# A two-layer graph network on one core: when x is loaded, and in how many transfers x, z and the output move

## The chip, the cores and the metric

The kernel runs on one core of one Trainium2 chip. The metric is the device time of one execution in microseconds. The time of a kernel is the median of several runs. Profiles come from one further execution that the hardware profiler records, and that execution can be longer than the timed ones.

## The reference, cut to what matters

There are 32 batches of x, each of 512 nodes by 512 features in float32, and one adjacency matrix `adj` of 512 x 512 for all of them.

```python
h = relu(layernorm(x))
x = x + einsum('nm,bmd->bnd', adj, h) @ W0 + b0          # layer 0
h = relu(layernorm(x))
q, k, v = h @ Wq + bq, h @ Wk + bk, h @ Wv + bv            # 8 heads of 64
scores = q @ k.T / 8 + (1 - adj) * -1e9                    # layer 1
x = x + (softmax(scores) @ v) @ Wo + bo
```

The mask of layer 1 uses weighted edges: an entry of `adj` that is not exactly 1 costs up to 1e9. So each row's softmax is, in float32, a choice of the one node with the largest entry, unless two entries are nearly equal. The kernel tests this at the start on the chip and takes `single_path` when it holds, `general_path` otherwise. The profile shows `single_path`.

## The kernel before, in words

In `single_path` layer 1 becomes: for each node take the row of h of the node that its mask selects, and multiply it by the folded weight Wv Wo (`wvo`). Many nodes select the same one, so only the distinct selected rows are computed, at most 352 (`32 * S`, S = 11).

Each 512 x 512 product is done by `product`, a Strassen-Winograd scheme of seven block products. Their pieces are named p1, p5, u2, c11, c22, c12, c21, in that order. A piece is four matmuls into a PSUM bank (line 287), and after each piece a `take` function moves the bank on: `take_onto` adds it to x on VectorE (line 344), `take_new` copies it on ScalarE (line 326) or adds it on VectorE (line 324), and `take_z` uses ScalarE (line 337) and VectorE (line 334). Pieces p1, u2, c22 and c21 share one bank, so c22 can't begin before u2 has been taken.

The order is written out by hand. For each b of the loop there are 21 steps, one for each piece of three products: steps 0 to 6 are layer 0 of batch b, steps 7 to 13 the aggregation with `adj` of batch b+1, and steps 14 to 20 layer 1 of batch b-1. `put(batch, step, f)` hangs a small piece of work on a step. All engines run in the order in which this loop emits their instructions, and an engine's queue stands still while its head waits.

Work around the change, for a batch n:

- `load_x` reads x of batch n into one of five buffers of x (`xs[n % 5]`), so batch n+5 needs the buffer of n after n was stored. It is issued by SyncE.
- `ln0` normalizes x for layer 0 (`stats` is line 194, `power` line 201 on GpSimd, `offset` line 204, `relu` line 212).
- After layer 0, the halves of x are normalized for layer 1 (steps 6 to 10), and `put_h` writes h to DRAM (`hs`, line 488, SyncE).
- `get_h` (line 494, GpSimd) gathers the listed rows of `hs` into `hc`, eleven indirect transfers: three at step 12 and eight at step 15, of which most run in the next pass of the loop.
- `transpose_h` (line 529) and `layer1` produce `zs`, the layer's output by columns.
- `put_z` transposes `zs` into `zr` on VectorE (line 545), in two parts, and SyncE writes each part to DRAM (`z`) in four transfers, one for each quarter of the partitions (line 549). Part (6, S) is put at step 20, part (0, 6) at step 0 of the next pass.
- `finish` (line 553, GpSimd) gathers for each node its row of `z` and adds it to x in the transfer itself, four indirect transfers at step 1.
- `store` (line 559) writes x to the output at step 12, in four transfers.

A tile framework adds the semaphores. The transfers of SyncE use eight semaphores in turn, and each transfer waits until the one eight places before it, which had the same semaphore, has landed. A reader of a tile waits for all the transfers that wrote it.

At the end, batch 31's layer 1 is done for all its rows by `layer1_rows` (lines 507 to 523). The last `finish` and the store of batch 30, issued by ScalarE, close the program.

Of the kernel before, what the change touches and what calls it, by code (L numbers as in the profile page):

```python
# [17 lines left out]
P = 128  # L18
# [8 lines left out]
def gnn_two_layers(ctx: ExitStack, tc: tile.TileContext, x, adj, w0, b0, wq, bq, wk, bk, wv, bv, wo, bo, out):  # L27
# [149 lines left out]
    with tc.If(single > P - 1) as cmp:  # L177
        single_path(tc, x, wv, bv, wo, bo, out, kept)
# [38 lines left out]
def single_path(ctx: ExitStack, tc: tile.TileContext, x, wv, bv, wo, bo, out, kept):  # L217
# [14 lines left out]
    nc = tc.nc  # L232
    B, N, D = x.shape
    C, DC = N // P, D // P
# [12 lines left out]
    X, H0 = {0: xs[0], 1: xs[1]}, {0: hs[0], 1: hs[1]}  # L247
    H0S, H1, HS, HC, HT, HTS, Z, ZT, ZR = {}, {}, {}, {}, {}, {}, {}, {}, {}

    def load_x(b):  # L250
        X[b] = xs[b % 5]
        for c in range(C):
            nc.sync.dma_start(X[b][:, c, :], x[b, c * P:(c + 1) * P, :])


    def blk(t, chunks, cols, half=HALF):
# [284 lines left out]
    def put_z(b, s0, s1):  # L541
        if b not in Z:
            Z[b] = dram.tile([32 * S, D], F32, name="z")
            ZR[b] = work.tile([P, S, P], F32, name="zr")
        nc.vector.transpose(ZR[b][:, s0:s1, :].rearrange("p s (c e) -> p s c e", c=4),
                            ZT[b][:, :, 32 * s0:32 * s1].rearrange("p c (s j) -> p s c j", j=32))
        rows = Z[b].rearrange("(s j) (q f) -> q j s f", j=32, q=4)
        for q in range(4):
            nc.sync.dma_start(rows[q][:, s0:s1, :], ZR[b][32 * q:32 * q + 32, s0:s1, :])

    def finish(b):
        for c in range(C):
# [1 line left out]
                out=X[b][:, c, :], out_offset=None, in_=Z[b],  # L554
                in_offset=bass.IndirectOffsetOnAxis(ap=place[:, c:c + 1], axis=0), compute_op=ALU.add)

    def store(b, eng=nc.sync):
        for c in range(C):
            eng.dma_start(out[b, c * P:(c + 1) * P, :], X[b][:, c, :])

    def run(steps, work_by_step):
        if steps is None:
# [16 lines left out]
    with tc.manual_schedule():  # L579
# [6 lines left out]
        for b in range(B + 1):  # L586
            todo = [[] for _ in range(21)]

            def put(batch, step, f, *args):
                if 0 <= batch < B:  # L590
                    todo[step].append(lambda: f(batch, *args))

            put(b - 2, 15 if b == B - 1 else 1, finish)
            put(b + 2, 2, load_x)
            for step, i in ((0, 0), (1, 1), (2, 2), (3, 3)) if b > 0 else ((1, 0), (2, 1), (2, 2), (3, 3)):
                put(b + 1, step, h0_sum, i)
            put(b - 2, 14 if b == B - 1 else 0, put_z, 0, 6)
            if b == B - 1:
                put(b - 2, 13, put_z, 6, S)
# [22 lines left out]
            if b < B - 1:  # L622
                put(b - 2, 12, store)
            elif b == B:
                put(b - 3, 1, store)
# [13 lines left out]
            if b < B and b != B - 2:  # L639
                put(b - 1, 20, put_z, 6, S)  # L640
# [36 lines left out]
                run(layer1(b - 1) if b < B and b != B - 2 else None, todo[14:21])  # L677
        layer1_rows(B - 1)
        if B > 1:
            store(B - 2, nc.scalar)  # L680


@with_exitstack
# [261 lines left out]
```

## Time and profile before

| what | value |
|---|---|
| time, median of 3 runs | 1118.38 us (1115.33 to 1119.31) |
| span of the profiled execution | 1168.3 us (its time: 1170.05 us) |
| TensorE matmul / VectorE / ScalarE / GpSimd busy | 94% / 78% / 31% / 56% |
| mean granted TensorE clock | 0.984 |
| HBM read / written | 96.28 MB / 89.46 MB |
| DMA queue of SyncE | 102320 packets, 123.05 MB, 31.0% of the 16 engines' span |
| DMA queue of GpSimd | 29472 packets, 56.47 MB, 27.4% |

A busy share is averaged over the whole span. The profile's chain follows back, from the last instruction, what each one waited for. In a timeline each row is a run of equal instructions: start, length, engine, line, operation, what it writes and reads, and in brackets how long the engine was idle before it and what ended that. TensorE's ends are modelled. In a windows answer each row is one stretch, with the busy time of each engine, then the granted clock, the mean busy share of the 16 DMA engines, and GB/s.

For one batch in the middle (it begins at 564.5 us of the span), SyncE's timeline is: eight transfers of z from 565.11, four of x from 568.95, two of hs from 582.78, four of the output from 585.31.

### The profile page before, as it was taken

How to read it: one execution, taken by the hardware profiler on the slowest of the kernel's cores; microseconds unless marked ns; L12 is line 12 of the kernel's file. 1: busy time of each engine (PE TensorE's matmuls, PEld its weight loads, DVE VectorE, ACT ScalarE, POOL GpSimd, SP SyncE). 2: the span in 40 equal slices, each digit the busy share in tenths (PEclk: the TensorE clock that was granted, in tenths of full speed). 3: DMA queues.
4: the chain of work that ended last, by engine and by line, in shares of the span. 5: the costliest groups of instructions: out<-in, count | busy, mean ns of one | idle time of the engine just before them, and what ended most of it. 6: DMA issues, size and time to landing. Idle time of an engine off the chain costs nothing.

```text
span 1168.3 us, 15855 instructions
## 1 busy us (share of the span) xinstructions
PE 1100.6 (94%) x5408; PEld 957.8 (82%) x5408; DVE 905.7 (78%) x1859; ACT 359.4 (31%) x655; POOL 653.9 (56%) x584
## 2 busy tenths in 40 slices
PE   7999989999989999999999999899999999999885
PEld 3658878989978989888989888798998889998782
DVE  6879868878867878787888888687887878887760
ACT  4223313233313233323323332223333232233120
POOL 2146536655646765565765555566565656666443
PEclk9999989999989999999999999999999999999998
DMA  6414665655666665576665657566566756666438
GB/s 225 153 19 129 165 173 140 171 170 149 168 173 139 165 180 147 153 191 167 150 177 171 159 155 187 133 170 178 155 165 172 190 140 167 180 176 156 120 118 203
DMA packets 135146, 186.90 MB, mean 160 GB/s; under 512 B 17472, under 2 KB 61120, under 8 KB 135056
## 3 DMA queue, kind: packets, MB, share of 16 engines
q1 hardware_dynamic: 102320, 123.05, 31.0%
q0 software_dynamic: 29472, 56.47, 27.4%
q10 hardware_dynamic: 3264, 6.29, 1.5%
q8 instruction: 44, 0.72, 0.2%
q14 instruction: 46, 0.38, 0.1%
HBM read 96.28 MB, written 89.46 MB: 159 GB/s over the span
## 4 chain that ended last, share of the span: by engine, by line
PE 83%; DVE 6%; issue 3%; POOL 3%; ACT 1%; DMA 1%; another core or an unknown queue 1%; SPq 0%; POOLq 0%; ACTq 0%; DVEq 0%
PE mm L287 78%; DVE x L344 2%; POOL x L553 1%; PE mm L139 1%; PE mm L480 1%; PE mm L371 1%; DVE st L194 1%; DMA x<-in_x_dram 1%; PE mm L520 1%; ACT h L212 1%; POOL rstd L201 1%; POOL hc L494 1%; DVE h0s L266 1%; DVE yT L324 0%
## 5 line engine op out<-in xcount | busy, mean ns | idle before, releaser
L494 POOL DMA_INDIRECT hc<-hs,listed x341 | 356.2, 1045 | 261.9 <-DMA hs<-h 157.2
L344 DVE TENSOR_TENSOR x<-mm,x 128x512 f32<-128x512 f32 x217 | 149.6, 690 | 146.6 <-PE mm L287 107.7
L326 ACT COPY yT<-mm 128x512 f32<-128x512 f32 x124 | 71.8, 579 | 614.3 <-PE mm L287 478.3
L553 POOL DMA_INDIRECT x<-z,place x124 | 196.0, 1581 | 70.2 <-issue 47.9
L287 PE MATMUL mm<-w_t,sel 128*128 128x256 f32 x744 | 182.2, 396 | 37.9 <-DVE x L344 31.6
L212 ACT ACTIVATE h<-x,off,rstd 128x512 f32<-128x512 f32 x256 | 194.7, 807 | 48.2 <-DVE off L204 46.3
L287 PEld LDWEIGHTS mm<-w_t,sel 128*128 128x128 f32 x744 | 143.9, 196 | 67.5 <-DVE x L344 39.4
L201 POOL TENSOR_TENSOR rstd<-ve,mhalf 128x2 f32<-128x2 f32 (+1 forms) x97 | 97.2, 1002 | 156.9 <-DVE ve L200 151.8
L194 DVE BATCH_NORM_STATS2 st<-x 128x6 f32<-128x512 f32 x256 | 171.6, 670 | 8.4 <-DMA x<-in_x_dram 7.3
L287 PE MATMUL mm<-adjT_s,h0s 128*128 128x256 f32 x744 | 170.9, 379 | 0.4 <-ACT yT L326 0.2
L287 PEld LDWEIGHTS mm<-adjT_s,h0s 128*128 128x128 f32 x744 | 141.2, 190 | 20.3 <-ACT yT L326 1.2
L287 PE MATMUL mm<-hTs,wvo_t 128*128 128x176 f32 x720 | 117.8, 313 | 1.7 <-ACT zs L337 1.7
L287 PE MATMUL mm<-w_s,yT 128*128 128x256 f32 x496 | 117.2, 379 | 0.0
L287 PE MATMUL mm<-adjT,h 128*128 128x256 f32 x496 | 117.2, 379 | 0.0
L337 ACT ACTIVATE zs<-mm,cvo_c 128x176 f32<-128x176 f32 x248 | 87.4, 404 | 94.7 <-PE mm L287 60.4
L287 PEld LDWEIGHTS mm<-hTs,wvo_t 128*128 128x128 f32 x720 | 109.7, 190 | 2.8 <-ACT zs L337 2.8
L287 PEld LDWEIGHTS mm<-adjT,h 128*128 128x128 f32 x496 | 94.2, 190 | 13.2 <-issue 0.5
L287 PEld LDWEIGHTS mm<-w_s,yT 128*128 128x128 f32 x496 | 93.1, 190 | 11.7 <-issue 0.5
L458 DVE TENSOR_TENSOR x<-x,b_r 128x512 f32<-128x512 f32 x128 | 86.5, 677 | 0.0
L287 PE MATMUL mm<-hT,wvo 128*128 128x176 f32 x480 | 81.4, 313 | 0.0
L287 PEld LDWEIGHTS mm<-hT,wvo 128*128 128x128 f32 x480 | 75.3, 190 | 1.5
L324 DVE TENSOR_TENSOR yT<-mm,yT 128x512 f32<-128x512 f32 x93 | 63.5, 682 | 4.1 <-PE mm L287 2.7
(152 smaller groups left out, 1262.9 us busy)
## 6 DMA issues: line engine op xcount, KB each, us to landing
hs<-h SPq DMA_DIRECT2D x64, 512.0 KB
out_dram<-x SPq DMA_DIRECT2D x124, 256.0 KB
x<-in_x_dram SPq DMA_DIRECT2D x120, 256.0 KB
z<-zr SPq DMA_DIRECT2D x124, 96.0 KB
z<-zr SPq DMA_DIRECT2D x124, 80.0 KB
hc<-hs,listed POOLq DMA_INDIRECT x341
x<-z,place POOLq DMA_INDIRECT x124
x<-in_x_dram ACTq DMA_DIRECT2D x4, 256.0 KB
```

The lines of the kernel that those rows point to most:

```text
L139: nc.tensor.matmul(ps, hs[0][:, m, d * P:(d + 1) * P], adjT[:, m, :], start=(m == 0), stop=(m == C - 1))
L194: self.nc.vector.bn_stats(st, self.src[:, self.chunks[i], :])
L201: self.nc.gpsimd.tensor_tensor(self.rstd, ve, self.mhalf[:, 0:n], ALU.pow)
L212: self.nc.scalar.activation(dst, src, AF.Relu, bias=self.off[:, i:i + 1], scale=self.rstd[:, i:i + 1])
L287: nc.tensor.matmul(bank[:, m, 0:half], lhs[:, k, m * P:(m + 1) * P], rhs[:, k, :], start=(first and m == 0 and k == 0), stop=(k == 1), ski ...
L324: nc.vector.tensor_add(dst, bank, dst)
L326: nc.scalar.copy(dst, bank)
L337: nc.scalar.activation(dst[:, m, :], bank[:, m, :], AF.Identity, bias=cvo_c[:, 2 * i + m:2 * i + m + 1])
L344: nc.vector.tensor_add(dst, bank, dst)
L458: nc.vector.tensor_add(X[b][:, c, :], X[b][:, c, :], b0_r)
L494: nc.gpsimd.indirect_dma_start(out=HC[b][:, s, :], out_offset=None, in_=HS[b].rearrange("n (q d) -> (n q) d", q=4), in_offset=bass.Indirec ...
L553: nc.gpsimd.indirect_dma_start(out=X[b][:, c, :], out_offset=None, in_=Z[b], in_offset=bass.IndirectOffsetOnAxis(ap=place[:, c:c + 1], axi ...
```

## The change

Three things change, all in transfers that SyncE issues. No arithmetic changes.

- x of a batch is loaded at step 15 of pass b for batch b+3, behind the store of batch b-2, whose buffer it takes. Before, it was loaded at step 2 of pass b for batch b+2. Batches 2 and 3 are still loaded at step 2 of passes 0 and 1.
- A load of x, and a store of the output, is one transfer of 1 MB instead of four of 256 KB. The last store, by ScalarE, keeps four (`store_rows`).
- z is written in four transfers of 176 KB, after the second transpose, instead of four of 80 KB after the first and four of 96 KB after the second.

It is meant to read x at a time when the transfers are few, to have it long before it is needed, and to have fewer transfers and fewer semaphores to wait for.

```diff
     def load_x(b):
         X[b] = xs[b % 5]
-        for c in range(C):
-            nc.sync.dma_start(X[b][:, c, :], x[b, c * P:(c + 1) * P, :])
+        nc.sync.dma_start(X[b], x[b].rearrange("(c p) d -> p c d", p=P))
...
-        rows = Z[b].rearrange("(s j) (q f) -> q j s f", j=32, q=4)
-        for q in range(4):
-            nc.sync.dma_start(rows[q][:, s0:s1, :], ZR[b][32 * q:32 * q + 32, s0:s1, :])
+        if s0 == 0:
+            for q in range(4):
+                nc.sync.dma_start(Z[b].rearrange("(s j) (q f) -> q j s f", j=32, q=4)[q], ZR[b][32 * q:32 * q + 32])
...
-    def store(b, eng=nc.sync):
-        for c in range(C):
-            eng.dma_start(out[b, c * P:(c + 1) * P, :], X[b][:, c, :])
+    def store(b):
+        nc.sync.dma_start(out[b].rearrange("(c p) d -> p c d", p=P), X[b])
+
+    def store_rows(b):
+        for c in range(C):
+            nc.scalar.dma_start(out[b, c * P:(c + 1) * P, :], X[b][:, c, :])
...
-            put(b + 2, 2, load_x)
+            if b < 2:
+                put(b + 2, 2, load_x)
+            if b > 0:
+                put(b + 3, 15, load_x)
...
-            store(B - 2, nc.scalar)
+            store_rows(B - 2)
```

## The prediction

> **What bounds the kernel now.** I read the page's busy shares first, then the chain of waits, then the timelines of PE, POOL and SP over single batches, last the windows of one batch for the DMA share.
>
> ```profile
> PE 1100.6 (94%) x5408; PEld 957.8 (82%) x5408; DVE 905.7 (78%) x1859; ACT 359.4 (31%) x655; POOL 653.9 (56%) x584
> ...
> PE 83%; DVE 6%; issue 3%; POOL 3%; ACT 1%; DMA 1%; another core or an unknown queue 1%; SPq 0%; POOLq 0%; ACTq 0%; DVEq 0%
> ```
>
> TensorE is the bound: 94% busy and 83% of the chain. DMA is 1% of the chain, so no transfer sets the end directly. A change of transfers can only win what TensorE loses in waits. How much is that? One batch of the steady state is layer 0 of b, aggregation of b+1 and layer 1 of b-1. In the PE timeline a batch begins where w_s,yT follows layer 1:
>
> ```profile
> 216.60 1.89 PE L287 MATMUL mm<-w_s,yT 128*128 128x256 f32 x8
> ...
> 249.14 1.89 PE L287 MATMUL mm<-w_s,yT 128*128 128x256 f32 x8
> ...
> 258.58 3.00 PE L287 MATMUL mm<-w_t,sel 128*128 128x256 f32 x8 [2.37 <-DVE x L344]
> ...
> 285.99 1.89 PE L287 MATMUL mm<-w_s,yT 128*128 128x256 f32 x8
> ```
>
> Batch 5 takes 249.14 - 216.60 = 32.54 us and has no PE gap: that is the floor. Batch 6 takes 36.85 us, with a gap of 2.37 us at c22, which waits until DVE has taken u2 (L344). Batch 1 starts at 74.66 and batch 31 at about 1103.8. The 29 whole batches between would need 29 x 32.54 = 943.7, and batch 30, which has no layer 1, about 24.2: 967.9 in all, against 1029.1 in the trace. So 61 us of the profiled run are waits. But that run took 1170.05 us where the timed ones took 1118.4. Taking out the waits gives 1170.05 - 61.2 = 1108.9, so the timed runs can hold only some 9.5 us of such waits, 0.3 us a batch, if start and end are the same. Most of the L344 waits seem to belong to the profiled execution. This 9.5 us is the most that the loop can give.
>
> The waits that may be left are found in the loop through GpSimd. It is nearly as long as the batch:
>
> ```profile
> 570.19 0.95 POOL L494 DMA_INDIRECT hc<-hs,listed  x1 [0.31 <-issue]
> 572.60 1.58 POOL L553 DMA_INDIRECT x<-z,place  x1 [1.46 <-DMA x<-in_x_dram]
> 574.49 1.55 POOL L553 DMA_INDIRECT x<-z,place  x1 [0.30 <-issue]
> 576.34 1.54 POOL L553 DMA_INDIRECT x<-z,place  x1 [0.30 <-issue]
> 578.19 1.53 POOL L553 DMA_INDIRECT x<-z,place  x1 [0.30 <-DVE ve L200]
> 579.18 1.29 POOL L201 TENSOR_TENSOR rstd<-ve,mhalf 128x2 f32<-128x2 f32 x1
> ...
> 588.43 1.05 POOL L494 DMA_INDIRECT hc<-hs,listed  x1 [5.37 <-DMA hs<-h]
> ```
>
> In batch 15 (from 564.6) the eleven gathers of hc end at 571.14, the four of finish follow, and behind them in POOL's order stands rstd (L201), whose input ve was ready at 577.98. From rstd the path goes to off, relu, hs, its landing, the gathers at 588.43 and so back to finish. ACT shows how tight it is:
>
> ```profile
> 580.76 0.81 ACT L212 ACTIVATE h<-x,off,rstd 128x512 f32<-128x512 f32 x1 [1.38 <-DVE off L204]
> 581.48 0.57 ACT L326 COPY yT<-mm 128x512 f32<-128x512 f32 x1
> 581.95 0.81 ACT L212 ACTIVATE h<-x,off,rstd 128x512 f32<-128x512 f32 x1
> 582.66 0.57 ACT L326 COPY yT<-mm 128x512 f32<-128x512 f32 x1
> ```
>
> The take of u2 (582.66 to 583.23) stands behind the relu that waited for rstd, and c22 of the aggregation begins at 583.77: 0.5 us of slack. The reader is to see that 0.5 us more at finish reaches TensorE, and that finish waits 1.46 us (0.3 would be its plain spacing) for z.
>
> **Where the DMA engines are full.** Windows of the same batch (DMA share and GB/s are the last two columns):
>
> ```profile
> 564.45:567.45 3.00, 3.00 (x17) 2.66 (x16) 3.00 (x5) 0.71 (x2) 2.08 (x4) 1.00 0.42 110
> 567.45:570.45 3.00, 3.00 (x16) 2.64 (x15) 1.66 (x3) 0.00 (x0) 2.39 (x3) 1.00 0.86 222
> 570.45:573.45 3.00, 3.00 (x15) 2.40 (x14) 1.98 (x3) 0.00 (x0) 1.54 (x2) 1.00 1.02 316
> ...
> 590.00:597.16 7.16, 7.16 (x51) 7.16 (x50) 6.87 (x15) 5.05 (x10) 6.03 (x6) 1.00 0.18 47
> ```
>
> z is written and x read at 0.86 to 1.02 of the engines, just when finish waits, while during layer 1 they stand at 0.18. The change carries 1 MB from the full stretch to the empty one.
>
> **What the Trainium skill says.** "DMA: Bandwidth & Descriptors", Anatomy of one DMA: about 2 us of each transfer are fixed, most of it the receipt of the write, HBM being slowest. The trace agrees roughly: the last z issue begins at 568.47, and finish was held until after 571.14. "Perfetto Trace Analysis", Tensor Engine Instruction: the end of a matmul in a profile is an estimate from its size. That fits: PE stands back to back while DVE waits for its result for 2 us and more. "TensorE: Matmul & The Clock Gate", HAM oscillation: an idle stretch can halve the clock for a window. The mean granted clock of 0.984 shows a little of it, so a wait of TensorE removed may save somewhat more than itself.
>
> **The change part by part.**
>
> Load of x. Of b+2 at step 2 before; of b+3 at step 15 after, so some 20 us earlier for each batch. DVE's waits for x are 7.3 us in 5 places, all before 22 us, where this load plays no part. The earlier arrival is worth 0 by itself. The load now stands behind the store whose buffer it takes (b+3 and b-2 share one of five), so SyncE waits there for the store to land. Behind it in SyncE's order is only z of the next batch, due 13 us after the store is issued (585.3 to about 599). A store of 1 MB behind hs took until about 590, and 1 MB of x at the 320 GB/s of the third window takes another 3.3 us: done near 594. Cost 0. It crosses the hc gathers of layer 1, paced by GpSimd at 1.25 us each, with 8 us until their transpose needs them: 0.
>
> One transfer for x and one for output. Six issues of 0.45 us fewer on SyncE, whose time is free: 0. The four stats wait for all of x instead of a quarter: 0 with 20 us in hand. The store waits for all four finish gathers; the last is issued at 578.19 and has landed well before the store at 585.3: 0.
>
> Four for z. Before, issues run from 565.11 (after the first transpose of zr) to 568.91. After, the first can go only when the second transpose ends, 566.55, and the fourth at about 566.6 + 3 x 0.45 = 568.0, done at 568.4: 0.5 us sooner than the eighth. The data, 704 KB, are 1408 packets of 512 B; the packet records have a median of 27 ns for these (84 for 2 KB), so 88 x 27 ns = 2.4 us on 16 engines alone and about 3.0 beside the hc gathers. From a first packet near 567.5 this ends at 570.5, and lands near 571; before, it was paced by the issues. So z is ready between 0.5 us earlier and, if the burst runs at the pace of before (704 KB at about 160 KB/us, 4.4 us), 1.0 us later. I take 0.3 us earlier. GpSimd then also waits for four z semaphores instead of eight, two waiting instructions of 0.09 us fewer. With x no longer filling the engines, the gathers of finish and their receipts are quicker. Together finish starts about 0.5 us sooner, which is as much as the 0.3 us a batch that the loop can give. I take 0.25 us x 29 = 7 us.
>
> The end. z of batch 30 is the last long link: eight issues from 1137.51 to 1142.3, held up by lanes and by finish of batch 29, then 4.99 us of idle on POOL before finish at 1149.29, and the stores follow. With four issues from 1138.92 to about 1140.7 the last is 1.6 us sooner; the engines are full there, so I take 1.3. Sum: 1118.4 - 7 - 1.3 = 1110.
>
> **The rivals.**
>
> Hidden anyway. x was never late and finish is not what TensorE waits for in timed runs; only the end gains, 1118.4 - 1.3 = 1117. For it: DMA is 1% of the chain, and the lost time of the trace stands at L344, which names PE and DVE, no transfer. Batch 30 loads no x and still has a c22 gap (3.45 us at 1084.74), so x is not its cause. Against it: the tight loop above.
>
> Slower: the burst of z. z starts 1.5 us later and lands 1.0 us later; finish, rstd, relu and the takes all move, and beyond 0.5 us of slack TensorE waits: 0.4 us x 29 = 12 us less the 1.3 of the end, 1129. A milder form, 0.2 us a batch, gives 1123. For it: z is the first link of that path and the first half loses its head start. Against it: the issues, not the engines, paced z before (0.42 and 0.86 of the engines).
>
> Much faster: the L344 waits of the profile are in timed runs too and come from full DMA engines. 61 us would be at stake, but 1118.4 leaves room for 9.5; the lowest time I believe is 1108.9 - 1.3 - some start effects, about 1102 to 1107.
>
> **How the numbers follow.** Forecast 0.45 and much faster 0.05, both faster; hidden 0.27; burst 0.23, most of it over 0.5% slower. Faster by over 0.5% is under 1112.8, slower is over 1124.0. Hence 0.5, 0.27, 0.23. The range is 1102 to 1127: below, all waits gone; above, half the weight of the burst is still inside.
>
> **What would show it.** In the profile after: the idle before the first finish gather falls from about 1.3 to under 1 us and DMA share in layer 1 rises from 0.18 to about 0.6; stats still wait for no x; POOL's idle at the end falls from 4.99 to about 3.5. L344 waits may stay, since they are the profiled run's. I am wrong if finish starts later than 8 us after the batch's begin, if rows of adjT_s,h0s wait for ACT yT, or if the L344 waits vanish and the timed run falls under 1102.

## The result, and the profile after

The kernel after takes 1123.81 us (median of 4 runs, 1122.38 to 1124.36), the kernel before 1118.65 us beside it. The ratio is 1.005, with an interval of 1.0028 to 1.0073: slower by half a per cent. A second measurement (f1 below) gave 1.0055 (1.0042 to 1.0068). The ratios and intervals in this document leave out executions that took over 1.5% more than the fastest of their kernel, which concerns the runs named e and one execution of h3, while each time is the median of all.

The profile before can't be laid beside the profile after as it stands. It is of an execution of 1170 us, when the timed ones took 1118; the profile after (span 1122.6 us) agrees with its timed runs. A further profile of the kernel before, called g1 (1114.3 us, span 1112.6), has the level of the timed runs, so the comparison is made with g1. It is a single execution at the quick end of them. The kernel after is one line shorter above `product`, so its L286, L325, L343 and L552 are L287, L326, L344 and L553 of the kernel before.

The page of after, its busy shares and its chain by engine, and the chain of g1:

```profile
PE 1089.8 (97%) x5408; PEld 950.7 (85%) x5408; DVE 904.9 (81%) x1859; ACT 359.0 (32%) x655; POOL 662.2 (59%) x584
...
PE 73%; DVE 13%; POOL 6%; DMA 3%; issue 3%; ACT 1%; SPq 0%; POOLq 0%; ACTq 0%; DVEq 0%
```

```profile
PE 82%; DVE 8%; POOL 4%; issue 2%; DMA 1%; ACT 1%; SPq 1%; ACTq 0%; POOLq 0%; DVEq 0%
```

TensorE is still the bound, 97% busy. But the chain passes through it less (73% against 82% in g1), and more through DVE, POOL and DMA: other engines set more often when TensorE goes on. One batch from TensorE's timeline, batch 15 again:

```profile
540.71 1.89 PE L286 MATMUL mm<-w_s,yT 128*128 128x256 f32 x8
...
573.73 1.89 PE L286 MATMUL mm<-w_s,yT 128*128 128x256 f32 x8
```

It takes 33.02 us, 0.48 more than the floor of 32.54. The median of the 29 batches is 33.01 (32.69 in g1). So most batches are a little late; the latest takes 34.17 us. What starts it, as the runs below show, is z. SyncE's timeline of this batch:

```profile
542.68 2.45 SPq L548 DMA_DIRECT2D z<-zr  x4
```

The first z issue is 1.97 us after the batch's begin, where before it was 0.51 us after it. The windows of the batch show what the DMA engines do then (DMA share and GB/s last), in after and then in g1:

```profile
540.70:543.70 3.00, 3.00 (x16) 2.67 (x15) 3.00 (x5) 0.70 (x2) 2.16 (x3) 1.00 0.18 53
543.70:546.70 3.00, 3.00 (x15) 2.64 (x15) 2.12 (x4) 0.00 (x0) 2.47 (x2) 1.00 0.93 230
546.70:549.70 3.00, 3.00 (x16) 2.65 (x15) 1.53 (x4) 0.00 (x0) 2.08 (x2) 1.00 0.34 88
566.10:573.26 7.16, 7.16 (x50) 7.16 (x49) 6.88 (x15) 5.08 (x11) 5.88 (x6) 1.00 0.68 204
```

```profile
536.40:539.40 3.00, 3.00 (x16) 2.64 (x15) 3.00 (x5) 0.70 (x2) 2.19 (x3) 1.00 0.47 124
539.40:542.40 3.00, 3.00 (x15) 2.66 (x14) 2.12 (x5) 0.00 (x0) 2.43 (x2) 1.00 0.90 216
542.40:545.40 3.00, 3.00 (x15) 2.64 (x14) 1.53 (x4) 0.00 (x0) 2.66 (x2) 1.00 0.96 297
561.90:569.06 7.16, 7.16 (x50) 7.16 (x49) 6.83 (x14) 5.05 (x10) 5.76 (x6) 1.00 0.13 41
```

x has gone to layer 1, as meant: 0.68 of the engines there, where it was 0.13. The third stretch of the batch has fallen from 0.96 to 0.34. But the first has fallen too, from 0.47 to 0.18, and z now fills the second at 0.93: the engines stand nearly empty while z is held back for the second transpose, and then all of z has to pass at once. By the semaphore records of this batch z's four transfers land 4.37, 5.54, 6.22 and 7.52 us after its begin; in g1 the last of eight lands at 6.43. Over all batches the medians of the last landing are 7.19 and 6.88 us. GpSimd's timeline shows the consequence:

```profile
546.78 1.42 POOL L493 DMA_INDIRECT hc<-hs,listed  x1 [0.30 <-issue]
549.04 1.58 POOL L552 DMA_INDIRECT x<-z,place  x1 [0.84 <-issue]
550.93 1.55 POOL L552 DMA_INDIRECT x<-z,place  x1 [0.30 <-issue]
552.78 1.54 POOL L552 DMA_INDIRECT x<-z,place  x1 [0.30 <-issue]
554.63 1.53 POOL L552 DMA_INDIRECT x<-z,place  x1 [0.30 <-DVE x L343]
555.62 1.29 POOL L201 TENSOR_TENSOR rstd<-ve,mhalf 128x2 f32<-128x2 f32 x1
```

The gathers of `hc` are over at 548.20. `finish` could follow at the plain spacing of 0.30 us, and starts 0.54 us later than that. The bracket says "issue", but z is what it is held for: its last transfer has landed 0.81 us earlier. The same stretch of the kernel before, in g1 (batch from 536.38):

```profile
542.44 1.43 POOL L494 DMA_INDIRECT hc<-hs,listed  x1 [0.30 <-issue]
544.17 1.58 POOL L553 DMA_INDIRECT x<-z,place  x1 [0.31 <-DMA x<-in_x_dram]
...
549.76 1.53 POOL L553 DMA_INDIRECT x<-z,place  x1 [0.30 <-DVE ve L200]
550.74 1.31 POOL L201 TENSOR_TENSOR rstd<-ve,mhalf 128x2 f32<-128x2 f32 x1
```

In this batch of g1 there is no wait for z at all. In the next one there is:

```profile
577.49 1.59 POOL L553 DMA_INDIRECT x<-z,place  x1 [1.10 <-DMA x<-in_x_dram]
```

(The bracket names x, whose transfers use the same semaphores; z's last transfer has landed 0.85 us earlier.) Of the 28 batches with a `finish`, 13 in g1 wait for z beyond the plain spacing, 7.0 us in all; in after all 28 do, 13.3 us in all. The wait of 1.46 us in the profile before came of an execution in which the gathers of `hc` ended earlier in the batch (6.5 us after its begin, not 7.5). Behind the four gathers stands rstd (L201). DVE had written its input ve at 553.91 in the batch of after, and it begins at 555.62 (its record overlaps that of the last gather; spans of GpSimd are rough). The Trainium skill says why ("PSUM — Partial Sum Buffer", Engine vs sequencer instructions): GpSimd's queue is a strict FIFO. The trace agrees; these 1.7 us are the gathers ahead of it (1.2 in the batch of g1). ScalarE's timeline carries the delay on:

```profile
557.20 0.81 ACT L212 ACTIVATE h<-x,off,rstd 128x512 f32<-128x512 f32 x1 [1.89 <-DVE off L204]
557.91 0.56 ACT L325 COPY yT<-mm 128x512 f32<-128x512 f32 x1
558.38 0.81 ACT L212 ACTIVATE h<-x,off,rstd 128x512 f32<-128x512 f32 x1
559.10 0.57 ACT L325 COPY yT<-mm 128x512 f32<-128x512 f32 x1
```

and so do the weight loads of TensorE (PEld):

```profile
559.72 1.59 PEld L286 LDWEIGHTS mm<-adjT_s,h0s 128*128 128x128 f32 x8 [0.25 <-ACT yT L325]
561.33 1.70 PEld L286 LDWEIGHTS mm<-adjT,h0s 128*128 128x128 f32 x8
563.54 1.59 PEld L286 LDWEIGHTS mm<-adjT_s,h 128*128 128x128 f32 x8 [0.51 <-DVE yT L323]
```

The take of u2, at 559.10, stands behind the relu that waited 1.89 us (1.35 in the batch of g1), and piece c22 waits for it. How closely TensorE follows can be read from after alone: batches in which `finish` begins at 7.90, 8.41 and 9.44 us take 32.58, 33.11 and 34.17 us. Over its 28 batches each microsecond by which `finish` begins later goes with 0.92 us more of batch. The waits of the whole run, total us, times, longest, in after:

```profile
ACT h L212 <- DVE off L204: 78.5, 64, 3.0
DVE off L204 <- POOL rstd L201: 61.2, 66, 2.2
...
PEld mm L286 <- DVE yT L323: 12.3, 29, 1.9
...
PEld mm L286 <- ACT yT L325: 7.6, 14, 1.4
```

and in g1:

```profile
ACT h L212 <- DVE off L204: 71.0, 64, 3.2
DVE off L204 <- POOL rstd L201: 54.3, 66, 2.4
...
PEld mm L287 <- DVE yT L324: 6.9, 13, 1.9
PEld mm L287 <- ACT yT L326: 4.3, 6, 1.6
...
PEld mm L287 <- DVE x L344: 1.8, 3, 1.2
```

The waits of TensorE's weight loads for the two takes grow from 11.2 to 19.9 us: 8.7 us more, while the 29 batches together grow from 952.4 to 958.4, by 6.0; so a late weight load doesn't hold up the matmuls by all of its wait.

### The profile page after: what moved, and what is told of

Same layout as the page of the kernel before. It is cut to its first block, busy times and chain, and to the rows that moved or that the text cites. A ratio compares the mean times of both kernels' runs of the same rounds, so it can differ in the third digit from the quotient of the medians.

```text
span 1122.6 us, 15439 instructions
## 1 busy us (share of the span) xinstructions
PE 1089.8 (97%) x5408; PEld 950.7 (85%) x5408; DVE 904.9 (81%) x1859; ACT 359.0 (32%) x655; POOL 662.2 (59%) x584
## 4 chain that ended last, share of the span: by engine, by line
PE 73%; DVE 13%; POOL 6%; DMA 3%; issue 3%; ACT 1%; SPq 0%; POOLq 0%; ACTq 0%; DVEq 0%
PE mm L286 69%; DVE st L194 4%; POOL x L552 3%; POOL rstd L201 2%; DVE yT L323 2%; DMA z<-zr 2%; PE mm L139 2%; DVE x L343 1%; PE mm L479 1%; POOL hc L493 1%; DVE mv L195 1%; DVE hT L528 1%; PE mm L370 1%; DMA hc<-hs,listed 1%; DVE zs L333 1%
## 5 line engine op out<-in xcount | busy, mean ns | idle before, releaser
L493 POOL DMA_INDIRECT hc<-hs,listed x341 | 367.3, 1077 | 261.5 <-DMA hs<-h 156.8
L325 ACT COPY yT<-mm 128x512 f32<-128x512 f32 x124 | 71.4, 576 | 545.4 <-PE mm L286 424.2
L552 POOL DMA_INDIRECT x<-z,place x124 | 192.9, 1555 | 58.6 <-issue 40.5
L343 DVE TENSOR_TENSOR x<-mm,x 128x512 f32<-128x512 f32 x217 | 149.6, 690 | 86.5 <-PE mm L286 86.5
L286 PE MATMUL mm<-adjT_s,h0s 128*128 128x256 f32 x744 | 172.1, 381 | 3.0 <-ACT yT L325 2.8
L201 POOL TENSOR_TENSOR rstd<-ve,mhalf 128x2 f32<-128x2 f32 (+1 forms) x97 | 104.9, 1081 | 114.0 <-DVE ve L200 111.5
L286 PE MATMUL mm<-w_t,sel 128*128 128x256 f32 x744 | 171.1, 380 | 0.8 <-DVE x L343 0.8
L286 PEld LDWEIGHTS mm<-adjT_s,h0s 128*128 128x128 f32 x744 | 140.6, 190 | 25.7 <-ACT yT L325 7.6
L286 PEld LDWEIGHTS mm<-w_t,sel 128*128 128x128 f32 x744 | 141.4, 190 | 20.5 <-DVE x L343 1.8
L286 PE MATMUL mm<-hTs,wvo_t 128*128 128x176 f32 x720 | 117.3, 313 | 0.6 <-ACT zs L336 0.6
L286 PE MATMUL mm<-w_s,yT 128*128 128x256 f32 x496 | 117.2, 379 | 0.0
L286 PE MATMUL mm<-adjT,h 128*128 128x256 f32 x496 | 117.2, 380 | 0.0
L286 PEld LDWEIGHTS mm<-hTs,wvo_t 128*128 128x128 f32 x720 | 109.8, 190 | 0.9 <-ACT zs L336 0.9
L286 PEld LDWEIGHTS mm<-adjT,h 128*128 128x128 f32 x496 | 94.5, 190 | 13.0 <-issue 0.5
L286 PEld LDWEIGHTS mm<-w_s,yT 128*128 128x128 f32 x496 | 93.3, 190 | 11.6 <-issue 0.5
L286 PE MATMUL mm<-hT,wvo 128*128 128x176 f32 x480 | 81.4, 313 | 0.0
L286 PEld LDWEIGHTS mm<-hT,wvo 128*128 128x128 f32 x480 | 75.3, 190 | 1.5
```

Of the source, the lines that this page charges most:

```text
L201: self.nc.gpsimd.tensor_tensor(self.rstd, ve, self.mhalf[:, 0:n], ALU.pow)
L286: nc.tensor.matmul(bank[:, m, 0:half], lhs[:, k, m * P:(m + 1) * P], rhs[:, k, :], start=(first and m == 0 and k == 0), stop=(k == 1), ski ...
L325: nc.scalar.copy(dst, bank)
L343: nc.vector.tensor_add(dst, bank, dst)
L493: nc.gpsimd.indirect_dma_start(out=HC[b][:, s, :], out_offset=None, in_=HS[b].rearrange("n (q d) -> (n q) d", q=4), in_offset=bass.Indirec ...
L552: nc.gpsimd.indirect_dma_start(out=X[b][:, c, :], out_offset=None, in_=Z[b], in_offset=bass.IndirectOffsetOnAxis(ap=place[:, c:c + 1], axi ...
```

## The experiments

Theory: z begins later, so it lands later, and through `finish`, rstd and the relus each batch becomes longer. Rivals: the move of x costs (it takes the engines from something in layer 1), or the single transfers of 1 MB cost (readers wait for all of it). The first four kernels take the change apart.

**e1 and f4: only the load of x moves**, in its four transfers.

```diff
-            put(b + 2, 2, load_x)
+            if b < 2:
+                put(b + 2, 2, load_x)
+            if b > 0:
+                put(b + 3, 15, load_x)
```

> The load of x moved to step 15 of the pass, for b+3, but in four transfers as before; output in four, z in eight as before. Theory Z (the burst of four z transfers lands late and holds finish, rstd and the takes): z is as before, so no loss; with x out of the way of z, 1113 to 1119 us. Rival X (x of 1 MB beside the hc gathers of layer 1 slows GpSimd's gathers and so the loop): slower, 1122 to 1126. Rival S (single transfers of x and output are the loss): 1117 to 1120.

> Only the load of x moved, in four transfers. Theory Z at a level of 1118 us of before: 1113 to 1119; at a level of 1179: 1160 to 1172. If x beside the hc gathers is the loss: slower than before by 4 us or more at the level of 1118.

**e2 and f2: only z goes in four transfers**, the kernel before otherwise.

```diff
-        for q in range(4):
-            nc.sync.dma_start(rows[q][:, s0:s1, :], ZR[b][32 * q:32 * q + 32, s0:s1, :])
+        if s0 == 0:
+            for q in range(4):
+                nc.sync.dma_start(Z[b].rearrange("(s j) (q f) -> q j s f", j=32, q=4)[q], ZR[b][32 * q:32 * q + 32])
```

> Only z in four transfers after the second transpose; x and output as before. Theory Z: most of the loss or more, 1122 to 1130 us, since x also stands close behind z here; the first gather of finish begins 0.4 us or more later in its batch than with eight. Rivals X and S: as before, 1116 to 1120.

> Only z in four. Theory Z at a level of 1118 us of before: 1122 to 1130; at a level of 1179: 1158 to 1168 as in the first run. Theory that x's move or the single transfers cause the loss: no difference from before at the level of 1118.

**e3 and h4: only x and the output go in single transfers.**

```diff
-        for c in range(C):
-            nc.sync.dma_start(X[b][:, c, :], x[b, c * P:(c + 1) * P, :])
+        nc.sync.dma_start(X[b], x[b].rearrange("(c p) d -> p c d", p=P))
...
+    def store(b):
+        nc.sync.dma_start(out[b].rearrange("(c p) d -> p c d", p=P), X[b])
...
```

> Only x and output in one transfer each, x at step 2 as before and z in eight. Theory Z and rival X: as before, 1116 to 1120 us. Rival S: slower, 1122 to 1126.

> Only x and output in one transfer each. If the single transfers neither cost nor gain: within 0.2% of before. If they delay h's landing or z: slower by 2 us or more. If fewer waits help: faster by 2 us or more.

**e4 and f3: the kernel after with z in eight transfers again**, each part issued after its own transpose.

```diff
-        if s0 == 0:
-            for q in range(4):
-                nc.sync.dma_start(Z[b].rearrange("(s j) (q f) -> q j s f", j=32, q=4)[q], ZR[b][32 * q:32 * q + 32])
+        rows = Z[b].rearrange("(s j) (q f) -> q j s f", j=32, q=4)
+        for q in range(4):
+            nc.sync.dma_start(rows[q][:, s0:s1, :], ZR[b][32 * q:32 * q + 32, s0:s1, :])
```

> The changed kernel with z back in eight transfers. Theory Z: the loss is gone, 1112 to 1118 us, finish begins at 7.4 to 8.0 us of a batch. Rivals X and S: still 1122 to 1126.

> The changed kernel with z in eight. Theory Z at a level of 1118 us of before: 1112 to 1118; at a level of 1179: 1158 to 1166. If x's move or the single transfers cause the loss, it is as slow as the changed kernel at the level of 1118.

**f1: the kernel after, unchanged**, beside f2 to f4.

> The changed kernel once more, beside the kernel before on the same chip. Its times are to say whether the chip or the hour sets the level: before measured 1118 us in the first comparison and 1179 us beside the first four experiments. Theory Z: where the kernel before takes about 1118 us, this is slower by 4 to 7 us (z burst); where it takes about 1179 us, most of the time lost is TensorE's late results in layer 0, and this one is faster, about 1150 to 1165. If the first comparison was only chance, ratio within 0.3% of 1 in both.

The e runs fell on a chip on which the kernel before took 1179.42 us (single runs 1161 to 1196), the others on two chips where it took 1116.71 to 1117.38.

| edit | e: us, ratio | f or h: us, ratio |
|---|---|---|
| x moved | 1166.75, 0.985 (0.979 to 0.991) | 1113.67, 0.9962 (0.995 to 0.9975) |
| z in four | 1161.94, 0.9885 (0.9836 to 0.9934) | 1136.81, 1.0178 (1.0165 to 1.0191) |
| single transfers | 1167.62, 0.996 (0.9926 to 0.9994) | 1117.65, 1.001 (1.0003 to 1.0018) |
| after, z in eight | 1161.22, 0.9884 (0.9837 to 0.9931) | 1114.36, 0.9974 (0.9963 to 0.9984) |
| after | not run | 1123.27, 1.0055 (1.0042 to 1.0068) |

The e runs don't answer the question: there each part alone is faster than before, by 0.4 to 1.5%, with wide spreads. At that level something else takes part in the time. TensorE waits for x's takes, as the waits of e2 show (a weight load and the matmul behind it can wait for the same take, so the two lines don't add up):

```profile
PEld mm L287 <- DVE x L344: 33.5, 16, 2.8
PE mm L287 <- DVE x L344: 27.0, 15, 2.4
```

In g1 these waits are nearly gone: its line above has 1.8 us.

The f and h runs answer it. From 1117.02, the move of x takes 3.3 us off; the single transfers on top of it add 0.7 (1113.67 to 1114.36), and alone 0.9; z in four adds 8.9 on top of both (1114.36 to 1123.27). The sum is +6.3. Neither rival explains the loss. And z in four on the kernel before costs 19.8 us, over twice as much. There x's load is issued right behind z, at 4.5 us of the batch, and z's last landing has its median at 7.80 us, against 7.21 in f1; that x and z share the engines is the likely reason.

**g1: the kernel before, profiled once more**, and **g2: z in eight, all issued after the second transpose, the (6, S) part first** (of the kernel after).

```diff
-            for q in range(4):
-                nc.sync.dma_start(Z[b].rearrange("(s j) (q f) -> q j s f", j=32, q=4)[q], ZR[b][32 * q:32 * q + 32])
+            rows = Z[b].rearrange("(s j) (q f) -> q j s f", j=32, q=4)
+            for t0, t1 in ((6, S), (0, 6)):
+                for q in range(4):
+                    nc.sync.dma_start(rows[q][:, t0:t1, :], ZR[b][32 * q:32 * q + 32, t0:t1, :])
```

> The kernel before, looked at again, for its profile on this chip. At a time of about 1118 us TensorE's c22 no longer waits for VectorE's take of u2 (under 5 us in all, against 71 in the first profile), z lands at about 6 us of a batch and finish begins at 7.8 to 8.0.

> The changed kernel, z in eight transfers again, but all eight issued behind the second transpose. If the later begin is what costs (the first half loses its head start), this is no better than four: 1123 to 1130 us where before takes 1117, z landed at 7.2 us or later. If the size of the transfers costs (176 KB moves slower than 80 and 96), this is as fast as eight early, 1113 to 1117.

g2 took 1113.5 us (0.9967, 0.9956 to 0.9979), the same as f3. Its begin didn't move: its first four transfers still begin 0.51 us after the batch's begin, since they read only what the first transpose wrote, and that is all that they wait for. Writing an issue later in the program delays nothing where its queue was idle. Hence:

**h1: the same, with the (0, 6) part first**, whose data is the later one, so that all eight wait for the second transpose.

```diff
-            for t0, t1 in ((6, S), (0, 6)):
+            for t0, t1 in ((0, 6), (6, S)):
```

> The changed kernel with z in eight transfers, the four of the second transpose first, so that all begin when the second transpose has ended. If the later begin costs: first issue at 2.0 us of the batch, last at about 5.4, landed at 7.5 us or later, 1123 to 1132 us where before takes 1117. If the size of the transfers costs: landed at about 6.5, 1113 to 1118.

h1 took 1141.25 us (1.022, 1.0207 to 1.0233). Its eight transfers differ from g2's in their order alone, and begin at 1.97 us of the batch rather than 0.51; that costs about 28 us (1113.5 to 1141.25, in two measurements). The last issue moves with the first, from 3.87 to 5.41 us. So the loss comes of the late begin, not of the small number. Starting late, four are better than eight (1123 against 1141): eight need 3.88 us to issue, and the last lands at 7.77 us of batch 15. GpSimd in h1 (batch from 548.42):

```profile
554.48 1.42 POOL L493 DMA_INDIRECT hc<-hs,listed  x1 [0.31 <-DMA z<-zr]
556.99 1.58 POOL L554 DMA_INDIRECT x<-z,place  x1 [1.09 <-issue]
```

The gap in front of `finish` has grown to 1.09 us.

**g3: the kernel after with z in eight, its second four issued by ScalarE**, so that two engines issue.

```diff
-        if s0 == 0:
-            for q in range(4):
-                nc.sync.dma_start(Z[b].rearrange("(s j) (q f) -> q j s f", j=32, q=4)[q], ZR[b][32 * q:32 * q + 32])
+        rows = Z[b].rearrange("(s j) (q f) -> q j s f", j=32, q=4)
+        eng = nc.scalar if s0 == 0 and b < B - 3 else nc.sync
+        for q in range(4):
+            eng.dma_start(rows[q][:, s0:s1, :], ZR[b][32 * q:32 * q + 32, s0:s1, :])
```

> x moved, single transfers of x and output, z in eight, the second four issued by ScalarE so that they need not stand behind the first four. Theory Z with the gathers of hc as the next bound (they end at 7.5 us, finish begins at 7.8): z lands a microsecond earlier, but finish can't begin earlier, so 1112 to 1115 us, the same as eight on one queue within 0.2%. If z were still the bound: 1108 to 1111.

g3 took 1112.76 us (0.9956, 0.9934 to 0.9977), 1.6 less than f3 in another measurement, with intervals of the ratios that overlap. z lands at 6.09 us of batch 15 (6.31 in f3), and `finish` was not waiting for it in the median batch. The Trainium skill expects no more ("DMA: Bandwidth & Descriptors", Issuing engines are not separate DMA queues): it puts the gain of a second issuing engine at the issuing time alone.

**g4: the kernel after, with the last gather of `finish` behind the first rstd.** If the path runs through rstd, z may land as late as it does, and the time must still fall.

```diff
-    def finish(b):
-        for c in range(C):
+    def finish(b, chunks=range(C)):
+        for c in chunks:
...
-            put(b - 2, 15 if b == B - 1 else 1, finish)
+            if b < B - 1:
+                put(b - 2, 1, finish, range(3))
+            else:
+                put(b - 2, 15 if b == B - 1 else 1, finish)
...
+            if b < B - 1:
+                put(b - 2, 6, finish, range(3, C))
```

> The changed kernel, z in four, but the last of finish's four gathers stands behind the first rstd of layer 1 on GpSimd instead of ahead of it. If the loss comes to TensorE through rstd standing behind finish, it goes: 1113 to 1118 us where before takes 1117 and the kernel after 1123. If z hurts by another way (DMA engines full, hc later), it stays at 1121 to 1126.

g4 took 1109.59 us (0.992, 0.99 to 0.9941). Its GpSimd timeline (batch from 532.71):

```profile
541.02 1.59 POOL L552 DMA_INDIRECT x<-z,place  x1 [0.83 <-issue]
542.92 1.56 POOL L552 DMA_INDIRECT x<-z,place  x1 [0.30 <-issue]
544.78 1.55 POOL L552 DMA_INDIRECT x<-z,place  x1 [0.30 <-issue]
546.08 1.00 POOL L201 TENSOR_TENSOR rstd<-ve,mhalf 128x2 f32<-128x2 f32 x1
547.26 1.58 POOL L552 DMA_INDIRECT x<-z,place  x1 [0.18 <-issue]
```

`finish` still waits 0.83 us for z. But rstd comes 13.37 us after the batch's begin, not 14.91, and the first relu at 548.03 waits 0.72 us for its offset, not 1.89. The waits of the run:

```profile
ACT h L212 <- DVE off L204: 36.9, 44, 2.6
DVE off L204 <- POOL rstd L201: 36.2, 43, 2.0
...
PEld mm L286 <- DVE yT L323: 1.9, 1, 1.9
```

Those for ACT yT are gone, and 27 of the 29 batches stand at the floor, although `finish` begins anywhere from 7.84 to 9.44 us of its batch, much as in after (7.86 to 9.44).

**h2: the same edit on f3, so with z in eight. h3: the same edit alone, on the kernel before.**

> x moved, single transfers, z in eight, and the last gather of finish behind the first rstd. If rstd behind finish is the only path of the loss: the loop is at its floor as with z in four and the same order, 1107 to 1111 us, no difference by z of over 0.2%. If z also costs by another way: 1104 to 1107.

> The kernel before, with only the last gather of finish behind the first rstd. If the kernel before loses its waits on that path too: 1108 to 1112 us where it takes 1117. If its waits come from x beside z in another way: 1114 to 1118.

h2 took 1109.94 us (0.9945, 0.9932 to 0.9958), h3 1109.59 us (0.9934, 0.992 to 0.9949). Five executions of h3 took 1106.37 to 1110.06 us; a sixth took 6572.54, is left out of the ratio, and has no trace that would tell why. With the gather behind rstd, it makes no difference that can be seen whether x and the transfers are as before (h3), as after (g4), or as after with z in eight (h2). All three beat both kernels, by 6.8 us and more. The dose can be read over the kernels, from their traces (us after a batch's begin, medians; z by the semaphore records):

| kernel | last z lands | `finish` begins | first rstd | 29 batches |
|---|---|---|---|---|
| g1, before | 6.88 | 7.80 | 14.40 | 952.4 |
| f4, x moved | 6.48 | 7.80 | 14.39 | 949.6 |
| f3, after, z in eight | 6.48 | 7.79 | 14.39 | 950.8 |
| f1, after | 7.21 | 8.09 | 14.68 | 957.8 |
| f2, z in four alone | 7.80 | 8.59 | 15.16 | 971.3 |
| h1, eight from 1.97 us | 7.78 | 8.65 | 15.21 | 972.6 |
| g4, after, gather behind rstd | 7.39 | 8.23 | 13.39 | 945.2 |
| h3, before, gather behind rstd | 7.01 | 7.94 | 13.37 | 945.4 |

Where `finish` waits for z it begins some 0.8 to 0.9 us after z's last landing, and in these kernels never before 7.79, where the gathers of `hc` let it. So z has slack until about 6.9 us of the batch. In f3 and f4 `finish` has no wait for z in 22 of 28 batches, in g1 in 15, in after and f1 in none. g4 and h3 are late in z and short in time.

## Why the prediction was wrong

It said 1110 us, and 1123.8 came: slower, where faster had the larger chance. Its rival "the burst of z", in the milder form of 0.2 us a batch and 1123 us, is what happened: from g1 to after the 29 batches grow by 6.0 us, 0.21 us each. That the number fits so closely is partly luck: it is a larger loss by z (8.9 us) less a gain by x (3.3 us) that the rival didn't have.

**The step that failed** is the term "Four for z": "z is ready between 0.5 us earlier and, if the burst runs at the pace of before (704 KB at about 160 KB/us, 4.4 us), 1.0 us later. I take 0.3 us earlier." The issues were worked out right: four between 1.97 and 3.44 us of the batch. The data were not. They were taken at 3.0 us on full engines. The first of the four landed at 4.37 us of batch 15 and the last at 7.52, so three transfers, 528 KB, took 3.15 us after it, 168 KB/us: about the pace of before, the slow end of the bracket (188 KB/us by the medians of all batches). Against g1, z came 1.1 us later in batch 15 (7.52 against 6.43) and 0.3 us later in the median (7.19 against 6.88), and `finish` 0.3 us later in the median (8.12 against 7.80), not the 0.5 us sooner of the forecast. The section of the Trainium skill that the prediction names for the fixed 2 us of a transfer describes those that GpSimd issues, while SyncE issues z; measured here, the first of the four (176 KB) lands 2.40 us after its issue, and the first of g1's eight (80 KB) 1.81 us.

**The slack.** The prediction gave the path 0.5 us before TensorE would notice, and let only what is beyond it count. The trace of after has next to none: `finish` at 7.90, 8.41 and 9.44 us, which is 0.11, 0.62 and 1.65 beyond 7.79, goes with batches 0.05, 0.58 and 1.64 us above the floor.

**The premise under it.** "Finish waits 1.46 us for z" was read in one batch of the profile of 1170 us. The text had itself found that this execution held 52 us that the timed ones don't, and discounted the L344 waits for it; it did not discount this wait. In g1 the median gap is 0.31 us, the plain spacing, but the median hides the rest: the 12 batches in which `finish` begins after 7.85 us hold 6.9 of the 8.5 us by which the 28 exceed the floor. So the premise was too large for a batch and yet right in kind: about the 7 us of the forecast could be had from a z that is in time in every batch. The change made it late in every batch. The measure "the most that the loop can give, 9.5 us" held: g1's 29 batches exceed the floor of 29 x 32.53 by 9.0 us, and h2, at the floor in 28 of 29, took 1109.94 us, where the prediction put the kernel without waits at 1108.9.

**L344 waits "belong to the profiled execution".** Right that runs at 1118 us hold next to none (1.8 us in g1). But they are no matter of profiling: all four e runs show them, e2 with 33.5 us in an execution of 1163.23 us among timed ones of 1159.59 to 1168.23. So they go with the slower level of that chip, and probably did in the profile before, whose chip is not on record. The same holds for the clock. In that profile the granted clock falls to half six times between 150 and 1090 us, for 3.4 or 6.8 us each; g1 has it full from 75 to 1080 us, so that in runs at 1118 us there was no clock to win back.

**x.** Moving it costs nothing, as predicted: DVE's waits for x are 8.4 us in six places, five of them in the first 23 us and one of 0.4 us at 94. It was priced at 0 by itself and gained 3.3 us (f4). With it z's last landing falls from 6.88 to 6.48 us in the median, and the batches in which `finish` waits for z from 13 to 6, which fits the expectation that x out of the way helps z and `finish`.

**Single transfers.** Predicted 0. Measured +0.9 us alone (1.001, 1.0003 to 1.0018): next to nothing, and not in favour.

**The end.** Predicted 1.3 us of gain. There is none: from the begin of batch 31 to the end after takes 63.9 us and g1 61.1. The chain of waits of after shows the last z there:

```profile
1091.87 1.72 DVE zr L544 x2
1094.45 0.76 SPq L548
1095.25 6.73 DMA z<-zr
1104.58 1.53 POOL x L552
```

The four issues are short, but they begin at 34.83 us of batch 31 where the eight of g1 begin at 32.58, and the last stands at 36.49 against 36.45: nothing is won. Then the landing takes 6.73 us from the last issue. Before the two `finish` stand gaps of 5.08 and 3.11 us, against 3.70 and 2.48 in g1. That the four standing in one burst cause this isn't shown: from the begin of batch 31 f3, with z in eight, still takes 63.0 us, and f4, where only x moves, 64.4.

**The signs named beforehand.** Two of the three signs of error came: `finish` later than 8 us (8.12 in the median), and rows of adjT_s,h0s that wait for ACT yT; the latter stand in g1 too (4.3 us under the weight loads), only fewer. Of the signs in favour the DMA share in layer 1 rose to 0.68 (about 0.6 was said), and the idle before the first gather of `finish` is under 1 us (0.64 in the median), but by luck: it fell because in after the gathers of `hc` end at 7.5 us of the batch and not at 6.5, and not because z came sooner. POOL's idle at the end didn't fall (5.08 us). The path itself, z, finish, rstd, relu, takes, was the right one, as g4 shows. What went wrong on it was the sign of one term, and the slack.

**What stays open.** Why TensorE's results come late on the one chip; no run here varies it. The kernel after wasn't run there, and its parts were each 0.4 to 1.5% faster there than before. Why the end is longer in f3 and f4 than in g1. Whether late z costs all that the chain shows through c22, or part of it through DVE's order (its takes stand behind the stats of x), wasn't separated.

## What to carry to other kernels

Fewer and larger transfers are worth nothing by themselves when the first of the smaller ones could start early: ask when the first byte can leave and when the last lands, not how many issues there are. The Trainium skill advises to coalesce into the largest transfer that one can ("SBUF — State Buffer", The DMA setup-cost knee); its case is a stream bound by bandwidth, and here, on a path bound by latency, four for eight cost 8.9 us. Where a small instruction feeds the critical path, look what stands ahead of it in its engine's queue: one gather moved behind rstd won more than all the transfers lost. And read a premise from an execution whose time is that of the timed runs, and over all its batches: neither one batch (1.46 us) nor the median (0.31) showed what z's lateness cost before the change.

## What the runs showed of the hardware that was not expected

- The level goes with the chip, or with the hour, which changed with it: the same kernel before took 1179.42 us on the chip of the e runs and 1116.71 to 1118.65 us in the other measurements. On the former, TensorE's weight loads wait for L344 (33.5 us in e2, 1.8 in g1), and z in four alone, which loses 1.8% elsewhere, gains 1.1% there.
- In the profile of 1170 us each fall of the granted clock to half begins during, or within 0.9 us after, a gap of TensorE of 2.3 us or more. Other gaps of that size have none (2.81 us at 949.9).
- z's transfers of 176 KB, issued within 1.5 us, land one after the other, the last three in 3.15 us in batch 15 (168 KB/us) and in 2.8 us by the medians, in the stretch with the DMA share at 0.93. In the layer 1 that follows, a window of 2 us with the 1 MB load of x in it shows 398 GB/s, at a share of 1.04.
- From the last landing of z to the first gather of `finish` that waited for it pass 0.81 us in f1, 0.76 in f2 and 0.93 in h1, in the median.
